# Attention, then gated attention: in Layer 1's first step, a block sum moved behind two evacuations and one group of values moved to another PSUM bank

## The chip, the core and the metric

The kernel runs on one core of a Trainium2 chip. The metric is the device time of one execution in microseconds, lower is better: before the change the median of three runs is 2317.9 us (2317.59 to 2318.22). Everything is computed in float32.

A core has a matrix engine (TensorE, "PE" in the profile, with its weight loads shown apart as "PEld"), a vector engine (VectorE, "DVE"), an activation engine (ScalarE, "ACT"), GpSimd ("POOL") and a sync engine ("SP") that here only issues DMAs. Matrix products are written to PSUM, which has eight banks; DVE and ACT read them out ("evacuate" them) to SBUF. Each engine works through its own list of instructions in order and waits at the first one whose inputs, or whose place to write, are not free.

## The reference

Eight images of 32 by 32 positions with 256 channels go through two layers.

```python
# layer 0, for each image: N = 1024 rows, C = 256, four heads
qkv = einsum('bnc,cd->bnd', xf, W_qkv)            # q, k, v for each head
atten = softmax(einsum('bihd,bjhd->bijh', q, k) * C ** -0.5, axis=2)
res = einsum('bijh,bjhd->bihd', atten, v)
x = einsum('bnd,dc->bnc', res, W_out) + b_out + xf
# layer 1, for each image: Ck = 32
f, g, h = x @ Wf + bf, x @ Wg + bg, x @ Wh + bh
o = softmax(g @ f.T, axis=-1) @ h
y = gamma * o + x
```

## The kernel before

**Tiling.** `P` is 128, `NB` 512 and `NBLK` 2: the 1024 rows of an image are worked in two blocks of 512 query columns. The loop over `steps` takes one step for every image, head and block of Layer 0, and for every image and block of Layer 1. `behind(b)` says where Layer 1 of image b-1 is put among the heads of image b: after two heads, and for the last image after all four. So seven of the eight images have the two Layer 1 steps in this loop; the last image's Layer 1 runs after it. The "first step of Layer 1" below is the step with `blk == 0`.

**Layer 0's products.** Scores, output products, projections and queries go through `seven`: a product of two matrices cut into two by two blocks is done with seven block products instead of eight. The sums of blocks that this needs are made ahead of time by `sum_a` (S1 to S4) and `sum_b` (T1 to T4), on DVE. `seven` returns three parts. The first does products 1, 6 and 5 into banks x, y and z and copies x to `e` (ACT); the second does products 2 and 7, copies x out (ACT), and adds `v` = y + e and output 22 = z + v (DVE); the third does products 4 and 3 on top of y and z and adds outputs 21 and 12 (DVE). The products add into the same banks from part to part, so that a part's products cannot start before the part ahead has read the bank.

**The projection** (`Layer0.project`, profile names ending in `_o`) uses `seven` with `two_banks=True`: x lies in one bank of the pool "psm", y and z share the other, each with 256 of its 512 columns. "psm" has two banks, so for as long as a projection is under way it holds both. All other banks, six, are the pool "ps", which scores, output products, queries and Layer 1's row products take turns in.

**Sums for the output products** (`Layer0.sums`): four pieces make S1 to S4 of the exponentiated scores, each 128 by 1024 elements on DVE. S2 and S4 share a place: S4 = a12 - S2 is written over S2, which product 6 reads in the first part of the output products; S4 itself is read by product 3, in their third part. Behind the pieces come four `keys`: three adds (L619) of S1's and S4's rows into `rs`, and `last`, one more add (L623), an all-reduce over partitions on POOL (L625) and two small DMAs on SP (`line`, L629, and `st`, L632). In a later step `invert` (L641) takes the reciprocal and sends it round through two more DMAs (L646 and L648) to become `invb`, by which the projection's outputs are multiplied (L699) before POOL adds them to `x1T` by DMA (L702).

**Layer 1's values** (`project_rows`, called by `Layer1.values`, names `pr_v_l`): four groups, each of eight matmuls of 128 by 256 into one bank, evacuated by one DVE instruction (L794).

**The order of the work.** For PE, DVE and ACT the order is written by hand: in each step, `put(tasks, *at)` collects tasks with a place number each, all of the step's tasks are sorted by it (those with the same number in the order in which they were put), and called. SP's and POOL's orders come from the framework's own scheduler. In a first step of Layer 1 the places around the change are these; "one" is the step before, "two" the step before that, both of Layer 0.

| place | task |
|---|---|
| 0 | third part of two's output products |
| 0.5, 2.4 | scores of this step, eight banks of "ps" in all |
| 0.8, 2.2, 3.5, 5.5 | S1, S2, S3, S4 of one |
| 1, 2.3, 3, 6.5 | the four groups of values |
| 1.1, 1.2, 1.3, 2.5 | block sums for two's projection |
| 2.5, 2.9, 4.2, 5.1 | transposes of Layer 1's rows (DVE, L394) |
| 4, 5 | first and second part of one's output products |
| 4.5, 6, 7.2 | the three parts of two's projection |
| 6.3, 7.6, 8.3, 8.7 | the keys of one |

The third part of one's output products is at 0 of the next step, Layer 1's second; there the scores follow at 0.5 and the first row product (`pa_l`, L899) at 1.

Of the kernel before, what the change touches and what calls it, by code (L numbers as in the profile page):

```python
# [16 lines left out]
P = 128  # L17
# [3 lines left out]
def kernel(  # L21
# [58 lines left out]
    NT = N // P  # L80
    NB = 512
# [29 lines left out]
    def tile_of(tag, shape, name):  # L111
        return pools[tag].tile(shape, F32, tag=tag, name=name)
# [244 lines left out]
    def transpose_rows(b, src, dst, layer):  # L357


        def task(k, c):  # L360
            if b not in dst:
                dst[b] = tile_of("xT", [P, CC, N], f"x{layer}T_{b}")
            pt = tile_of("psm", [P, NB], f"px{layer}_{b}_{k}_{c}")
            for t in range(HT):
                nc.tensor.transpose(
                    pt[:, ts(t, P)], src[b][:, k * HT + t, ts(c, P)], ident
                )
            nc.scalar.copy(dst[b][:, c, ts(k, NB)], pt)

        return [partial(task, k, c) for k in range(NBLK) for c in range(CC)]  # L370
# [50 lines left out]
    def key_sums(b):  # L421

        made = {}

        def piece(i):
            if i == 0:
                xT = xT_of[b]
                t = tile_of("v", [P, 4, HN], f"xs_{b}")
                sums = [t[:, k, :] for k in range(4)]
                blocks = [xT[:, c, ts(k, HN)] for k in range(2) for c in range(CC)]  # L430
                made["l"] = sum_a(sums, *blocks)
                xblocks[b] = a_operands(blocks, sums)
            made["l"][i]()

        return [partial(piece, i) for i in range(4)]
# [47 lines left out]
            partial(task, k, d) for k in range(NBLK) for d in range((width + P - 1) // P)  # L483
        ]

    def project_rows(name, w, src, evacuate):


        def task(t2):
            pm = tile_of("psm", [P, NB], f"pr_{name}_{t2}")  # L490
            for j in range(2):
                for c in range(CC):
                    nc.tensor.matmul(  # L493
                        pm[:, ts(j, C)],
                        lhsT=src()[:, c, ts(2 * t2 + j, P)],
                        rhs=w()[:, c, :],
                        start=(c == 0),
                        stop=(c == CC - 1),
                    )
            evacuate(t2, pm.rearrange("p (t c) -> p t c", c=C))  # L500

        return [partial(task, t2) for t2 in range(NT // 2)]

    def values_tile(name):
        return tile_of("v", [P, NT, CV], name)

    def ones(v):
        nc.gpsimd.memset(v[:, :, C : C + 1], 1.0)
# [208 lines left out]
    class Layer1:  # L717
# [65 lines left out]

            return [task], [partial(move, r) for r in range(quarters)]

        def values(self):
            def start():
                if self.v is None:
                    self.v = values_tile(f"v_{self.name}")
                ones(self.v)  # L790

            return [start] + project_rows(
                f"v_{self.name}", lambda: wh_sb, lambda: x1T_of[self.b],
                lambda t2, pm: nc.vector.scalar_tensor_tensor(  # L794
                    self.v[:, 2 * t2 : 2 * t2 + 2, :C], pm, gamma_sb,
                    bh_sb.unsqueeze(1).broadcast_to([P, 2, C]), ALU.mult, ALU.add,
                ),
            )

        def scores(self, blk):  # L800
# [144 lines left out]
    pm = tile_of("psm", [P, NB], "pm_idle")  # L945
# [6 lines left out]
    def behind(b):  # L952

        return 2 if b < B - 1 else HEADS
# [12 lines left out]
    turn_x, sums = transpose_rows(0, rows, xT_of, 0), key_sums(0)  # L967
# [5 lines left out]
    def is_l0(s):  # L973
        return s is not None and isinstance(s[0], Layer0)

    def step(k):
        return steps[k] if 0 <= k < len(steps) else None
# [4 lines left out]
    for i, (a, blk) in enumerate(steps):  # L982
        l0 = isinstance(a, Layer0)
        one, two, nxt = step(i - 1), step(i - 2), step(i + 1)
        places = []

        def put(tasks, *at):
            assert len(tasks) == len(at)
            places.extend(zip(at, range(len(places), len(places) + len(at)), tasks))

        if l0:
            put(a.scores(blk), 0, 2, 4, 6, 8, 10)
        else:
            tasks, _ = a.scores(blk)
            put(tasks, *((0.5, 2.4) if blk == 0 else (0.5, 2)))
        if is_l0(two):
            u, k = two
            put(u.products_of[k][2:], 1 if l0 else 0)
            if nxt is None:
                put([partial(u.invert_all, k)], 2.2)  # L1000
            put([partial(u.invert, k)], 3.4 if l0 else 2.7)
            ysums, tasks, adds[i] = u.project(k)
            put(ysums, *((1.1, 1.2, 1.3, 3.3) if l0 else (1.1, 1.2, 1.3, 2.5) if blk == 0 else
                         (0.6, 0.7, 0.8, 0.9)))
            put(tasks, *((3, 5.5, 7) if l0 else (4.5, 6, 7.2) if blk == 0 else
                         (3, 5, 7) if nxt else (1.9, 3.1, 4.1)))
            if nxt is None:
                put(adds[i], 4.2)
        if i - 1 in adds:
            put(adds[i - 1], 0.5 if l0 or blk == 1 else 2.3)  # L1010
        if is_l0(one):
            u, k = one
            sums, keys = u.sums(k)
            u.products_of[k] = u.products(k)
            put(sums, *((2.1, 3.2, 4.2, 5.6) if l0 else (0.8, 2.2, 3.5, 5.5)))
            put(keys, *((6.3, 6.6, 7.6, 8.7) if l0 else (6.3, 7.6, 8.3, 8.7)))
            put(u.products_of[k][:2], *((5, 9) if l0 else (4, 5)))
        elif one is not None:
            put(one[0].products(one[1]), *((3, 5, 7, 9) if l0 else (1, 4, 6, 8) if nxt else (1, 3, 4, 8.5)))
        if i == 0:  # L1020
            put(fold[0][2:] + fold[1], -2, -1, 0.5, 1.5, 2.5, 4.5, 6.5, 8.5)
            put(first_sums[:2], 8.4, 9.4)
        if i == 1:
            put(first_sums[2:], 1.4, 3.4)
            put(fold[2], 0.5, 2.6, 3.5, 5.5, 7.5)
            put([partial(nc.vector.tensor_scalar, bh_sb, bh_sb, gamma_sb, None, ALU.mult)], 8.5)

        if l0 and blk == 0:
            put(a.query_sums(1), 3.5, 4.3, 4.4, 5.3)
        if is_l0(nxt) and blk == NBLK - 1:  # L1030
            put(nxt[0].queries(), *((2.5, 4.5, 6.5) if not l0 else
                                    (1.5, 2.5, 4.5) if is_l0(two) else (0.5, 2.5, 5.5)))
            put(nxt[0].query_sums(0), *((6.7, 6.9, 7.3, 7.6) if not l0 else
                                        (5.4, 6.4, 7.2, 7.4) if is_l0(two) else (6.4, 7.2, 7.3, 7.4)))

        if l0 and a.h == 0 and blk == 1:
            put(residual(a.b), 5.3, 7.3)
        if l0 and a.h == 0 and blk == 1 and a.b > 0:
            put(value_sums(a.b), 1.4, 2.4, 3.4, 4.4)
        if l0 and a.h == 1 and blk == 0 and a.b + 1 < B:  # L1040
            load_x(a.b + 1)
        if is_l0(nxt) and nxt[0].h == 2 and nxt[1] == 0 and nxt[0].b + 1 < B:
            moves, turned = turn_rows(nxt[0].b + 1)
            put(moves[:4], 1, 2.5, 4, 5.5)
        if l0 and a.h == 2 and a.b + 1 < B:
            if blk == 0:
                put(moves[4:], 0.5, 1.5, 2.5, 3.5)
                put(turned, 6.4, 7.4, 8.4, 9.4)
            else:
                put(key_sums(a.b + 1), 0.5, 0.6, 6.4, 7.4)  # L1050

        if l0 and a.b > 0 and a.h == behind(a.b) - 1:
            if blk == 0:
                moves, turned1 = turn_back(a.b - 1)
                put(moves[:4], 3, 4.5, 6, 7.5)
            else:
                put(moves[4:], 4, 5.5, 7, 8.5)
                tasks, moves = nxt[0].queries_apart()
                put(tasks, 1.5)
                put(moves, 1.6, 1.7, 1.8, 1.9)  # L1060
        if not l0 and blk == 0:
            put(a.values(), 0.9, 1, 2.3, 3, 6.5)
            put(turned1, 2.5, 2.9, 4.2, 5.1)
        if nxt is None:
            fg = final.queries()
            moves, turned1 = turn_back(B - 1)
            put(moves, *[9.1 + 0.1 * k for k in range(8)])
        for _, _, t in sorted(places, key=lambda x: x[:2]):
            t()
# [90 lines left out]
    with tc.If(bad > 0), ExitStack() as general:  # L1160
# [7 lines left out]
        for b in range(B):  # L1168
# [3 lines left out]
            for h in range(HEADS):  # L1172
                a = General0(b, h, bout_sb)
# [4 lines left out]
            a = Layer1(b)  # L1178
# [37 lines left out]
```

## Time and profile before

| | us |
|---|---|
| median of three runs | 2317.9 |
| the profiled execution's own time | 2317.2 |
| its span on the core | 2315.4 |
| PE busy | 2302.4 (99%) |
| PE weight loads busy | 1892.5 (82%) |
| DVE busy | 1661.6 (72%) |
| ACT busy | 585.5 (25%) |
| POOL busy | 317.9 (14%) |
| seven instructions S4, one for each first step, mean of one | 1.2 |

The profile is one execution. "Busy" counts the time in which an engine has an instruction; the matmuls overlap, so PE's share says little about how well it is used. In the timeline, a line gives start, length, engine, source line, operation, what is written from what, shapes and count; neighbours of one kind are merged, and a bracket at the end tells how long the engine stood idle before and for whom. In a list of waits, a line gives the engine and its waiting line, whom it waited for, the total in us, how often, and the longest. Lines of helpers stand for many places: L255 is every product of `seven`, L272 every add of it, so the names of the tiles tell them apart (`_y` output products, `_o` projection, `_q` queries, no ending for scores).

### The profile page before, as it was taken

The numbers are of one execution on the slowest core, as the hardware profiler recorded it, in microseconds if no ns is written. First come the engines' busy times: TensorE is split into PE (matmuls) and PEld (weight loads), VectorE is DVE, ScalarE is ACT, GpSimd is POOL, SyncE is SP. The second block draws the span as 40 slices with busy tenths as digits, with TensorE's granted clock in tenths as the row PEclk, the third lists the DMA queues.
The fourth block names the chain that finished last, engine by engine and source line by source line (L and its number), as shares of the span: only waits on it lengthen the run. The fifth ranks groups of instructions, "written<-read, shape, count | busy, mean of one in ns | idle before, by whom it ended". The sixth has DMA issues, their size and how long they took to land.

```text
span 2315.4 us, 27268 instructions
## 1 busy us (share of the span) xinstructions
PE 2302.4 (99%) x10256; PEld 1892.5 (82%) x10256; DVE 1661.6 (72%) x2963; ACT 585.5 (25%) x1015; POOL 317.9 (14%) x199
## 2 busy tenths in 40 slices
PE   9999999999999999999999999999999999999999
PEld 7888887788878888788887888878888788888877
DVE  6787786577865777657776677766777667777765
ACT  2222222222221222212232122221222222222223
POOL 0111112011120112101121011210112101111210
PEclk9999999999999999999999999999999999999999
DMA  4211122301232012221132211321113210121222
GB/s 137 33 28 26 21 39 51 74 14 28 36 53 66 14 28 49 45 60 14 28 56 42 57 15 28 58 42 55 19 24 58 42 36 19 28 46 24 39 44 49
DMA packets 239740, 94.16 MB, mean 41 GB/s; under 512 B 204208, under 2 KB 208944, under 8 KB 239600
## 3 DMA queue, kind: packets, MB, share of 16 engines
q1 hardware_dynamic: 220400, 55.10, 12.2%
q0 software_dynamic: 19200, 37.23, 9.2%
q8 instruction: 83, 1.36, 0.4%
q14 instruction: 57, 0.47, 0.1%
HBM read 29.76 MB, written 8.65 MB: 17 GB/s over the span
## 4 chain that ended last, share of the span: by engine, by line
PE 98%; DVE 1%; issue 0%; ACT 0%; DVEq 0%
PE psy_y L255 14%; PE psy L255 14%; PE pa_l L899 10%; PE psx L255 10%; PE psz L255 10%; PE psx_y L255 10%; PE psz_y L255 10%; PE psy_o L255 6%; PE psy_q L255 4%; PE psx_q L255 2%; PE psz_q L255 2%; PE psx_o L255 2%; PE pr_v_l L493 2%; PE ps_l L811 1%; PE pm_fg L766 1%; DVE ss L612 0%
## 5 line engine op out<-in xcount | busy, mean ns | idle before, releaser
L625 POOL PARTITION_ALL_REDUCE rb<-rs x64 | 206.6, 3229 | 1450.8 <-DVE rs L623 910.1
L255 PE MATMUL psx<-q,x0T 128*128 128x256 f32 x1024 | 263.5, 380 | 0.0
L255 PE MATMUL psy<-qs,xs 128*128 128x256 f32 x1024 | 262.9, 379 | 0.0
L255 PE MATMUL psz<-q,xs 128*128 128x256 f32 x1024 | 262.8, 379 | 0.0
L575 ACT ACTIVATE p<-p 128x1024 f32<-128x1024 f32 x128 | 135.3, 1057 | 494.0 <-DVE p L272 494.0
L255 PE MATMUL psx_y<-p,x 128*128 128x256 f32 x1024 | 241.9, 379 | 0.0
L255 PE MATMUL psy_y<-p,xt 128*128 128x256 f32 x1024 | 241.9, 379 | 0.0
L899 PE MATMUL pa_l<-v_l,s_l 128*128 128x257 f32 x1024 | 231.5, 381 | 0.0
L255 PEld LDWEIGHTS psx<-q,x0T 128*128 128x128 f32 x1024 | 193.8, 190 | 45.3 <-issue 20.7
L255 PEld LDWEIGHTS psx_y<-p,x 128*128 128x128 f32 x1024 | 194.6, 190 | 34.1 <-issue 8.6
L899 PEld LDWEIGHTS pa_l<-v_l,s_l 128*128 128x128 f32 x1024 | 193.9, 190 | 32.9 <-issue 6.1
L255 PEld LDWEIGHTS psy<-qs,xs 128*128 128x128 f32 x1024 | 194.5, 190 | 26.8 <-DVE q L272 0.4
L255 PEld LDWEIGHTS psz<-q,xs 128*128 128x128 f32 x1024 | 194.6, 190 | 26.5
L255 PEld LDWEIGHTS psy_y<-p,xt 128*128 128x128 f32 x1024 | 194.6, 190 | 26.5
L284 ACT ACTIVATE p<-psx 128x512 f32<-128x512 f32 x128 | 76.5, 597 | 363.7 <-PE psx L255 363.5
L272 DVE TENSOR_TENSOR u<-psy,e 128x512 f32<-128x512 f32 x128 | 88.2, 689 | 87.0 <-ACT e L278 75.5
L702 POOL DMA_DIRECT2D x1T<-o x64 | 78.0, 1219 | 424.2 <-DVE o L699 301.8
L255 PE MATMUL psy<-qs,x0T 128*128 128x256 f32 x512 | 132.1, 380 | 0.3 <-DVE v L272 0.3
L272 DVE TENSOR_TENSOR v<-psy,e 128x512 f32<-128x512 f32 x128 | 88.3, 690 | 52.8 <-PE psy L255 51.3
L255 PE MATMUL psy_y<-ss,xt 128*128 128x256 f32 x512 | 121.4, 380 | 0.1
L255 PE MATMUL psz_y<-ss,x 128*128 128x256 f32 x512 | 121.0, 379 | 0.0
L255 PE MATMUL psz_y<-ss,xt 128*128 128x256 f32 x512 | 120.9, 379 | 0.0
(141 smaller groups left out, 3418.5 us busy)
## 6 DMA issues: line engine op xcount, KB each, us to landing
x1T<-o POOLq DMA_DIRECT2D x64, 512.0 KB, 5.0
invb<-inv SPq DMA_DIRECT2D x63, 256.0 KB
x<-x1T SPq DMA_DIRECT2D x256, 32.0 KB
out_dram<-x SPq DMA_DIRECT2D x15, 512.0 KB
x<-in_x_dram SPq DMA_DIRECT2D x14, 512.0 KB
x0T<-x SPq DMA_DIRECT2D x224, 32.0 KB
fg<-v_l POOLq DMA_DIRECT2D x56, 64.0 KB, 2.1
w<-in_L_conv_W_qkv_dram SPq DMA_DIRECT2D x4, 512.0 KB
```

The costliest lines, as they stand in the source:

```text
L255: nc.tensor.matmul(banks[k][:, ts(i, w)], lhsT=lhsT, rhs=rhs, start=first and n == 0, stop=True, skip_group_check=True,)
L272: nc.vector.tensor_tensor(dst, shaped(banks[k]), shaped(other), ALU.add)
L284: copy(outs["11"](), shaped(banks["x"]))
L493: nc.tensor.matmul(pm[:, ts(j, C)], lhsT=src()[:, c, ts(2 * t2 + j, P)], rhs=w()[:, c, :], start=(c == 0), stop=(c == CC - 1),)
L575: exp(both, both)
L625: nc.gpsimd.partition_all_reduce(t, r.rearrange("p e i -> p (e i)"), P, bass_isa.ReduceOp.add)
L702: nc.gpsimd.dma_start(x1T_of[self.b][:, :, ts(blk, NB)], o, accum_op=ALU.add)
L766: nc.tensor.matmul(pm[ts(k, half)], lhsT=w[:, c, :], rhs=x1T_of[b][:, c, ts(k, NB)], start=(c == 0), stop=(c == CC - 1),)
L811: nc.tensor.matmul(pm, lhsT=self.f[ts(r, CK), ts(j0 + r, P)], rhs=self.g[ts(r, CK), ts(blk, NB)], start=True, stop=True,)
L899: nc.tensor.matmul(pm[:, : C + 1], lhsT=p[:, j, ts(ti, P)], rhs=v[:, j, : C + 1], start=(j == 0), stop=(j == NT - 1),)
```

## The change

Three things change, in the first steps of Layer 1 only.

- S4 moves from place 5.5 to 6.1. It was ahead of the projection's second part (6) and is now behind it, ahead of the first of the keys (6.3).
- `project_rows` gets an argument `last`, the pool of its last group's bank, and `values` hands it on. Without it nothing is different.
- The loop's call of `values` gives "ps": the fourth group of values (place 6.5) takes one of the six banks of the scores instead of one of the two of "psm".

```diff
-    def project_rows(name, w, src, evacuate):
+    def project_rows(name, w, src, evacuate, last="psm"):
         def task(t2):
-            pm = tile_of("psm", [P, NB], f"pr_{name}_{t2}")
+            tag = "psm" if t2 < NT // 2 - 1 else last
+            pm = tile_of(tag, [P, NB], f"pr_{name}_{t2}")
...
-        def values(self):
+        def values(self, last="psm"):
...
                     bh_sb.unsqueeze(1).broadcast_to([P, 2, C]), ALU.mult, ALU.add,
-                ),
+                ), last,
             )
...
-            put(sums, *((2.1, 3.2, 4.2, 5.6) if l0 else (0.8, 2.2, 3.5, 5.5)))
+            put(sums, *((2.1, 3.2, 4.2, 5.6) if l0 else (0.8, 2.2, 3.5, 6.1)))
...
         if not l0 and blk == 0:
-            put(a.values(), 0.9, 1, 2.3, 3, 6.5)
+            put(a.values("ps"), 0.9, 1, 2.3, 3, 6.5)
```

The `put` of the sums is reached only where the step before is one of Layer 0, and of Layer 1's steps that is the first alone. The values of the last image, after the loop, and the kernel's general path, which runs only if a check of the sums fails, call without the argument and stay as they were.

## The prediction

> **What bounds the kernel now.** I read the page first, then the waits by engine, then the timeline of one first step of Layer 1 on TensorE, on its weight loads, and on VectorE. The page:
>
> ```profile
> span 2315.4 us, 27268 instructions
> PE 2302.4 (99%) x10256; PEld 1892.5 (82%) x10256; DVE 1661.6 (72%) x2963; ACT 585.5 (25%) x1015; POOL 317.9 (14%) x199
> ```
>
> TensorE (PE) has 13 us of the span not busy, and its waits are few. The list of waits, PE and its loads:
>
> ```profile
> PE psy_o L255 <- DVE o L272: 4.2, 7, 0.6
> PE pm_idle L947 <- DVE col L134: 1.1, 1, 1.1
> ...
> PEld psy_o L255 <- DVE o L272: 7.0, 7, 1.0
> ...
> PEld pr_v_l L493 <- ACT o L284: 3.0, 7, 0.4
> ```
>
> The largest wait comes seven times, once in each of the seven first steps of Layer 1 in the loop over steps. All seven look alike; I take the first (372 to 404 us). Columns: start, length, engine. PE, then its loads, then VectorE (DVE):
>
> ```profile
> 394.24 0.59 PE L255 MATMUL psx_o<-y,wvo 128*128 128x256 f32 x2
> 394.67 0.59 PE L255 MATMUL psy_o<-yt,wo 128*128 128x256 f32 x2
> 395.29 1.99 PE L493 MATMUL pr_v_l<-wh_sb,x1T 128*128 128x256 f32 x8
> 397.89 0.70 PE L255 MATMUL psy_o<-yt,wvo 128*128 128x256 f32 x2 [0.61 <-DVE o L272]
> 398.43 0.59 PE L255 MATMUL psy_o<-y,wo 128*128 128x256 f32 x2
> ```
> ```profile
> 395.29 1.59 PEld L493 LDWEIGHTS pr_v_l<-wh_sb,x1T 128*128 128x128 f32 x8 [0.43 <-ACT o L284]
> 397.89 0.30 PEld L255 LDWEIGHTS psy_o<-yt,wvo 128*128 128x128 f32 x2 [1.01 <-DVE o L272]
> ```
> ```profile
> 394.44 0.42 DVE L272 TENSOR_TENSOR v_y<-psy_y,e_y 128x256 f32<-128x256 f32 x1 [2.96 <-PE psy_y L255]
> 394.90 0.43 DVE L272 TENSOR_TENSOR y<-psz_y,v_y 128x256 f32<-128x256 f32 x1
> 395.24 0.70 DVE L394 STREAM_TRANSPOSE x<-x 128x512 f32<-128x512 f32 x1
> 395.86 1.18 DVE L612 TENSOR_TENSOR ss<-p,ss 128x1024 f32<-128x1024 f32 x1
> 396.97 0.41 DVE L272 TENSOR_TENSOR v_o<-psy_o,e_o 128x256 f32<-128x256 f32 x1
> 397.42 0.42 DVE L272 TENSOR_TENSOR o<-psy_o,v_o 128x256 f32<-128x256 f32 x1
> ```
>
> L612 at 395.86 is S4. It stands ahead of v_o and o, the two evacuations after the projection's second part. PE is in order: its third part (397.89) loads 0.05 us after the end of o (397.84).
>
> **What the Trainium skill says.** "PSUM — Partial Sum Buffer", section on bank collisions, says that PSUM is to be guarded by bank and quadrant, not by address. The trace agrees: the third part's first product writes only the y half, read by v_o (ended 397.38), yet is released by o, the reader of the z half of the same bank. "SBUF — State Buffer", section "Who interferes with whom", says that a VectorE instruction with two SBUF inputs contends with a GpSimd instruction that reads SBUF. The trace agrees: the multiply at 402.86 beside the all-reduce (401.78 to 405.01) took 2.23 us; most others take 1.22.
>
> **The change part by part.**
>
> *(a) S4 from 5.5 to 6.1.* It passes only what the projection's second part (at 6) issues: PE's four matmuls and ACT's copy are not in its queue; on DVE it passes v_o and o. It issues no DMA, and no SP or POOL instruction of its own stands between. Now v_o takes S4's slot, 395.86 (product 7 ended at 395.26); o follows 0.45 later as today, 396.31 to 396.73; PE may load at 396.78 instead of 397.89. S4's start-to-start time is 1.11 us (395.86 to 396.97), so o comes 1.11 us earlier.
>
> *(b) The last values' group in a bank of the scores.* The projection with two_banks holds both psm banks (x in one, y and z in the other). So the fourth group today waits until ACT has copied x out: its load comes 0.43 us late, its matmuls at 395.29 instead of 394.67 + 2 x 0.216 = 395.10. In a ps bank that wait goes; the new one is on that bank's last reader. Counting allocations in program order (the bank longest free is given), it is the bank of the sixth score block of this step, exponentiated by 384.6: over for 10 us. The next score blocks then get the four oldest free banks in shifted order; the values' own bank is the fourth, evacuated about 399.1 and wanted about 401.3. Cost nothing; the cover is 2 us.
>
> *(c) Sum.* PE's group of eight takes 8 x 0.216 = 1.73 (as every group of eight at 1.73 between starts), 395.10 to 396.83, so (b) lets PE arrive in time for o, and (a) sets the end: the load at 396.78, then the pair at 0.54 (397.89 to 398.43, a pair that starts without a preloaded weight; others 0.43). The pair ends its turn at 397.32 instead of 398.43: **1.11 us per step**. Alone, (a) would let PE go on at 397.12, where it is ready today: 0.77 to 0.88; (b) alone nothing, since o ends at 397.84 anyway. Upper end: all that is lost now, 0.19 + 0.10 (the group at 1.83) + 0.77 + 0.11 = 1.17. Seven steps: 7 x 1.11 = 7.8 us.
>
> *What is late next.* With PE 1.11 us earlier I check each thing it then meets; DVE has the same work, so its clock hardly moves.
> - S4 ends about 397.85; the product that reads it (400.59 now) comes at 399.48: 1.4 us of cover.
> - The first add of S4's rows now stands right behind S4 and depends on it: a dependent pair starts 0.46 apart (394.44, 394.90), an independent one 0.34, so DVE is about 0.12 later. The add out of psy_y, now 401.52, ends at 402.06; pa_l takes that bank, at 403.48 - 1.11 = 402.37. Cover 0.3 us. Without it PE would stand by what is missing, before each of seven steps.
> - The multiply by invb ends with the all-reduce, near 405.1, early or not. Four ysums and the first row's reciprocal and add follow, until about 407.5; psy_q, which by the same count of banks takes pa_l's, loads at 408.75 - 1.11 = 407.64. Cover 0.1. In the seventh step the projection comes sooner (2238.66 - 1.11 = 2237.55, ysum ended at 2237.51): some 0.1 to 0.2 us lost once.
> - DMAs do not follow PE: the sums' columns land at 412.4, invb at 431.8, and DVE stands for them (0.83 and 1.40 us today). Behind invb stands v (ends 433.66), for which PE loads at 435.32, then at 434.21: cover 0.55 in the first batch. In the other five v ends near 432.96 on the same scale (717.32 + 0.69 - 285.05): 1.2.
>
> So 7.8 less about 0.1: **7.7 us**. Profiled execution 2317.2 (span 2315.4 and 1.8 around it) becomes 2309.5; it stood 0.7 below the median of the runs, so the median 2317.9 becomes **2310.2**.
>
> **The rivals.**
>
> *B, part of the gain.* The waits' list of PE names only 0.61 us a step; taken so, 4.3 us, 2313.6. Against it: the loads' 1.01 and 0.43 are gaps of the same place, and PE's starts account for 1.17. Nearer is that a thin cover fails, pa_l's 0.3 or psy_q's 0.1: every missing tenth costs 0.7 us, and three tenths give 2312.3.
>
> *C, no change.* If the group were handed another bank than I count, the next scores could draw the bank of psz_y, which DVE empties only near 402.5, while PE wants it at 401.3: 1.2 us back per step, about 2318. For it: the trace shows no bank numbers. Against: the order of frees in the code leaves the four other banks older.
>
> *D, slower.* SP's order is not written by hand. The moves of the next x0T wait for the last values' group to let go of x1T (SP's first starts at 397.32, the group ends 397.28), and it now ends about 0.3 earlier. If more of them were put ahead of the sums' DMAs, invb would land later and PE stand at v. A move takes about 0.63 us of SP (3 in 1.89, 7 in 4.59). PE loses 6 x (delay - 1.1, the mean cover), and it is slower by over 0.2% when this exceeds 7.7 + 4.6, from a delay of 3.2 us, five moves. Eight moves, 5.0 us, cost 23.4: 2333.6. Against: SP now stands from 401.9 to 405.0 for the all-reduce; four or five moves that slip in there cost nothing.
>
> **How the numbers follow.** A measurement of this kernel tells 0.2%, 4.6 us, from no change. A, the forecast, 0.74 (2309.4 to 2311.2: 1.17 a step at one end, 0.95 at the other); B 0.14 (2311.2 to 2314, mostly still faster); C 0.08; D 0.04. Faster: 0.74 and 0.12 of B, 0.86; same: 0.10; slower 0.04. The range 2309.3 to 2313.0 holds A but its edges and most of B.
>
> **What would show it.** Right: PE's wait of psy_o for o gone or below 0.2 us a step; pr_v's wait for ACT gone; DVE in the order v_o, o, S4, first add, values; the distance from psx_o's second pair to the first pa_l in that step 1.1 us shorter, and the period of a batch (first pr_v to first pr_v) 283.95 instead of 285.07 us. Wrong: a new PE wait at pa_l (for y), at ps_l (for y or z), or at psy (for v) with a longer DVE wait for invb.

## The result, and the profile after

The changed kernel takes 2311.62 us (median of eight runs, 2311.16 to 2312.06); the kernel before, run beside it, took 2318.06 us. The ratio is 0.9974, with an interval of 0.9965 to 0.9983: 6.4 us faster, where 7.7 were forecast. The profiled execution took 2311.8 us, with a span of 2309.9.

The page of the kernel after:

```profile
span 2309.9 us, 27289 instructions
PE 2299.7 (100%) x10256; PEld 1891.9 (82%) x10256; DVE 1663.3 (72%) x2963; ACT 585.5 (25%) x1015; POOL 317.9 (14%) x199
```

The waits of PE, of its loads and of DVE, kernel after (total, times, longest). The diff moves the lines from 490 on down by one: L493, L612 and L699 of before are L494, L613 and L700 here.

```profile
PE psy L255 <- DVE v L272: 1.6, 4, 0.5
...
PEld psy L255 <- DVE v L272: 6.1, 12, 0.9
...
PEld psy_o L255 <- DVE o L272: 1.4, 7, 0.3
...
DVE o L700 <- DMA invb<-inv: 20.8, 6, 3.9
```

PE's wait of `psy_o` for `o`, 4.2 us in all before, is not in its list any more. In its place stands a small wait that hardly existed before (0.3 us, once): `psy`, a product of Layer 0's scores, for the evacuation `v`. And DVE stands 20.8 us for `invb`, not 4.5.

First, the place of the change: the timeline of the first step of Layer 1, kernel after.

```profile
393.72 0.59 PE L255 MATMUL psx_o<-y,wvo 128*128 128x256 f32 x2
394.15 0.59 PE L255 MATMUL psy_o<-yt,wo 128*128 128x256 f32 x2
...
394.58 1.89 PE L494 MATMUL pr_v_l<-wh_sb,x1T 128*128 128x256 f32 x8
394.72 0.70 DVE L394 STREAM_TRANSPOSE x<-x 128x512 f32<-128x512 f32 x1
395.34 0.39 DVE L272 TENSOR_TENSOR v_o<-psy_o,e_o 128x256 f32<-128x256 f32 x1
...
395.76 0.42 DVE L272 TENSOR_TENSOR o<-psy_o,v_o 128x256 f32<-128x256 f32 x1
396.11 1.22 DVE L613 TENSOR_TENSOR ss<-p,ss 128x1024 f32<-128x1024 f32 x1
396.24 0.30 PEld L255 LDWEIGHTS psy_o<-yt,wvo 128*128 128x128 f32 x2 [0.17 <-DVE o L272]
396.31 0.64 PE L255 MATMUL psy_o<-yt,wvo 128*128 128x256 f32 x2
```

The values' group starts 0.43 us after the pair before it, without a wait for ACT's copy; S4 stands behind `o`; the load of the third part comes 0.06 us after the end of `o` (396.18). That this first product, which writes only the y half, still goes by the reader of the z half agrees again with what the Trainium skill says in "PSUM — Partial Sum Buffer" on bank collisions. (The two halves are also slices of one tile of the program, and no run here tells a guard by bank from a guard by tile.) From this step's second pair of `psx_o` to its first `pa_l` it is 8.11 us (393.72 to 401.83); before it was 9.24 (394.24 to 403.48). Six of the seven steps show 8.11, one (the third) 8.27: 7.75 us in all, or 7.9 without the 0.16 that the third lost to a late transfer (see e1); 7.8 were forecast.

Now the place that gives some of it back, 38 us later in Layer 0. The timeline of the kernel before, DVE and PE, then that of the kernel after, DVE, PE and its loads:

```profile
431.84 1.23 DVE L699 TENSOR_TENSOR o<-o,invb 128x1024 f32<-128x1024 f32 x1 [1.40 <-DMA invb<-inv]
432.98 0.68 DVE L272 TENSOR_TENSOR v<-psy,e 128x512 f32<-128x512 f32 x1
...
435.53 1.03 PE L255 MATMUL psy<-qs,x0T 128*128 128x256 f32 x4
```
```profile
432.46 1.23 DVE L700 TENSOR_TENSOR o<-o,invb 128x1024 f32<-128x1024 f32 x1 [3.68 <-DMA invb<-inv]
433.61 0.68 DVE L272 TENSOR_TENSOR v<-psy,e 128x512 f32<-128x512 f32 x1
...
434.34 0.73 PEld L255 LDWEIGHTS psy<-qs,x0T 128*128 128x128 f32 x4 [0.70 <-DVE v L272]
434.35 0.91 PE L255 MATMUL psy<-qs,x0T 128*128 128x256 f32 x3 [0.30 <-DVE v L272]
```

DVE stands for `invb` with the multiply at the head of its list; `v`, which needs nothing of it, is queued behind, and PE's next `psy` waits for `v`. A batch is the stretch from one image's first group of values (`pr_v_l`) to the next one's; the table counts us from each first group on. The forecast's own numbers give 54.6 as the latest start of the multiply that costs nothing (load 434.21, less 0.05, less 1.82 from the multiply's start to the end of `v`, less 377.76). The same working with the figures of the profile after gives 54.65:

| batch | 1 | 2 | 3 | 4 | 5 | 6 |
|---|---|---|---|---|---|---|
| multiply by `invb` starts, before | 54.1 | 53.3 | 53.2 | 53.2 | 53.5 | 53.3 |
| the same, after | 55.22 | 54.77 | 55.58 | 54.35 | 55.36 | 54.99 |
| period, after, over the best of 283.93 (sixth: 404.74) | 0.57 | 0.11 | 0.92 | 0 | 0.71 | 0.33 |

The last row is the second less 54.65, where that is positive, to within 0.01. Its sum is 2.64 us, 0.16 of it in the projection of batch 3. The account of the two profiled executions: 7.9 gained, 2.6 lost here, 0.3 lost in the seventh step (below), 0.5 ahead of the loop's first group of values, which starts at 377.24 instead of 377.76: 5.5, as 2317.2 less 2311.8 gives 5.4. The 0.5 is not the change's: in the twelve profiles of this case that group starts between 377.1 and 378.3.

### The profile page after: what moved, and what is told of

Read it like the earlier page. It is cut to its first block, busy times and chain, and to the rows that moved or that the text cites. A ratio compares the mean times of both kernels' runs of the same rounds, so it can differ in the third digit from the quotient of the medians.

```text
span 2309.9 us, 27289 instructions
## 1 busy us (share of the span) xinstructions
PE 2299.7 (100%) x10256; PEld 1891.9 (82%) x10256; DVE 1663.3 (72%) x2963; ACT 585.5 (25%) x1015; POOL 317.9 (14%) x199
## 4 chain that ended last, share of the span: by engine, by line
PE 96%; DMA 3%; DVE 1%; SPq 0%; ACT 0%; issue 0%; DVEq 0%
PE psy_y L255 14%; PE psy L255 14%; PE psx_y L255 10%; PE psz_y L255 10%; PE psz L255 9%; PE psx L255 9%; PE pa_l L900 8%; PE psy_o L255 6%; PE psy_q L255 3%; PE pr_v_l L494 3%; PE psx_q L255 2%; PE psx_o L255 2%; PE psz_q L255 2%; DMA inv<-inverse 2%; PE ps_l L812 1%; DMA invb<-inv 1%
## 5 line engine op out<-in xcount | busy, mean ns | idle before, releaser
L272 DVE TENSOR_TENSOR v<-psy,e 128x512 f32<-128x512 f32 x128 | 88.3, 690 | 53.0 <-PE psy L255 51.7
```

Source lines behind the costliest of these rows:

```text
L272: nc.vector.tensor_tensor(dst, shaped(banks[k]), shaped(other), ALU.add)
```

## The experiments

Ten runs were made in three groups, e1 to e4, e5 to e8, and e9 with e10, each group on its own chip; e8 and e9 repeat the kernels before and after. Each ratio is to the kernel before in the same group. The theory: S4's place ahead of the evacuations sets PE's restart, the bank only lets PE get there in time, and what was missing went at `invb`. The rivals: the bank does the work; SP's order puts more transfers ahead of `invb`; the landing of `invb` differs by itself, with no edit, and the loss with it.

### One part alone

**e1**, S4 moved, the bank as before:

```diff
-            put(a.values("ps"), 0.9, 1, 2.3, 3, 6.5)
+            put(a.values(), 0.9, 1, 2.3, 3, 6.5)
```

> Only S4 moved (6.1); the last values' group stays in its psm bank. Theory (S4's place sets when PE may go on, the bank only keeps PE from being late for it): the values' group still starts 0.19 us late, PE is ready at its old moment, and the distance from psx_o's second pair to the first pa_l falls from 9.24 us to 8.36 (0.88 less; 1.13 less with both). Seven times 0.88 is 6.2 us, less what is given back at invb (0.2 to 0.4 a batch): about 2313. Rival (the bank brings a share of its own, the two add up): about 8.7, and the other 0.6 shows with the bank alone.

Measured: 2314.69 us, ratio 0.9983 (0.9976 to 0.9991), 1.7 us above the 2313 expected. Five steps show 8.37 us from `psx_o` to `pa_l`, 0.87 less than before. The other two show 8.52 and 9.22; together they lose 1.0 us of the gain, and two batches lose 1.0 us each at `invb`, more than the 0.2 to 0.4 expected. The third batch, kernel e1, PE and ACT:

```profile
965.70 0.37 ACT L284 COPY o<-psx_o 128x256 f32<-128x256 f32 x1 [2.64 <-DMA x1T<-o]
...
966.13 1.99 PE L494 MATMUL pr_v_l<-wh_sb,x1T 128*128 128x256 f32 x8 [0.89 <-ACT o L284]
```

ACT's copy out of `psx_o` writes `o`, which an earlier DMA (`x1T<-o`) still reads. With both banks of "psm" held, PE stands for that copy. In the kernel after the same copy came 3.36 us late, and the step lost only 0.16 us, since DVE's `o` waited 0.19 us for the same transfer. So the bank has a second use that the forecast did not name.

**e2**, the bank changed, S4 at 5.5 as before:

```diff
-            put(sums, *((2.1, 3.2, 4.2, 5.6) if l0 else (0.8, 2.2, 3.5, 6.1)))
+            put(sums, *((2.1, 3.2, 4.2, 5.6) if l0 else (0.8, 2.2, 3.5, 5.5)))
```

> Only the last values' group in a bank of the scores; S4 stays at 5.5. Theory: nothing, since o ends when it did: the distance stays at 9.24, the values' group starts 0.2 us earlier and PE's wait for o grows from 0.61 to about 0.9 us; time 2318. Rival (the two add up): the distance falls by 0.3 to 0.6 us, time 2314 to 2316.

Measured: 2319.50 us, ratio 1.0003 (0.9995 to 1.0012), and 9.23 to 9.25 us from `psx_o` to `pa_l`: nothing gained. (The time is 1.5 us above the 2318 expected; e4 says where that went.) PE's waits, kernel e2, show where its earlier arrival goes:

```profile
PE psy_o L255 <- DVE o L272: 6.3, 7, 0.9
```

PE finishes the values sooner and stands 0.9 us a step for the same `o`, not 0.6. S4 alone brings 0.87, the bank alone 0, and both together 1.13, as the forecast's working had it (0.77 to 0.88, 0, 1.11): the rival that the bank does the work is out.

### Another dose at the same place

**e5**, the kernel before with the fourth transpose of Layer 1's rows behind the evacuations, in place of S4:

```diff
-            put(turned1, 2.5, 2.9, 4.2, 5.1)
+            put(turned1, 2.5, 2.9, 4.2, 6.05)
```

> The kernel before, with the fourth transpose (0.62 us on DVE) moved behind the projection's second part, S4 left at 5.5. Theory (PE goes on when o ends, whatever stands ahead of it on DVE): o ends 0.62 us earlier, PE's wait for o of 0.61 goes, the distance from psx_o's second pair to the first pa_l falls from 9.24 to about 8.6; seven times 0.62 is 4.3 us, less 0 to 0.3 a batch at invb: 2314 to 2316. Rival (S4 itself is the hindrance, by what it locks or reads, not its length): 9.24 stays.

Measured: 2313.56 us, ratio 0.9985 (0.9978 to 0.9991), 8.64 us from `psx_o` to `pa_l`: 0.60 less. The transpose's start-to-start time is 0.62. PE restarts directly behind `o`, kernel e5:

```profile
396.64 0.42 DVE L272 TENSOR_TENSOR o<-psy_o,v_o 128x256 f32<-128x256 f32 x1
396.98 0.70 DVE L394 STREAM_TRANSPOSE x<-x 128x512 f32<-128x512 f32 x1
397.12 0.30 PEld L255 LDWEIGHTS psy_o<-yt,wvo 128*128 128x128 f32 x2 [0.41 <-DVE o L272]
```

Two different instructions, 1.11 and 0.62 us from start to start, moved across the same two evacuations, pay 1.13 (with the bank changed too, so that PE is there in time) and 0.60. That is what the step claims.

**e6**, both behind the evacuations, and the multiply by `invb` moved as in e3 below:

> The changed kernel with the multiplication by invb at 4.5 and also the fourth transpose behind the projection's second part. Theory: o now ends before PE is ready for it, so only the last 0.06 us a step is left to gain: distance 8.05, batch periods 283.87, about 0.4 us below the same without the transpose, 2309.2. Rival (PE still waits for DVE there): 0.6 us a step, 2305.

Measured: 2310.16 us, ratio 0.9970 (0.9959 to 0.9981). A miss: 8.18 us (8.51 in the third batch, where ACT's copy was late again), not shorter than 8.11. `psy_o`'s third part does not wait for `o` any more, but the next thin cover (the time by which a result is ready before it is wanted) is used up. Kernel e6, DVE and the loads:

```profile
402.42 0.42 DVE L272 TENSOR_TENSOR y<-psy_y,e_y 128x256 f32<-128x256 f32 x1
...
402.96 1.16 PEld L900 LDWEIGHTS pa_l<-v_l,s_l 128*128 128x128 f32 x6 [0.84 <-issue]
```

The add out of `psy_y` ends at 402.84 and `pa_l` loads 0.12 us later. This is the cover that the forecast put at 0.3 (in the kernel after the add ends at 401.56, 0.27 before `pa_l` at 401.83). The likely reason, read from the timeline and not tried: DVE has no more work to put between `y` (395.46) and `v_o` (395.99), which stands for its product, and so it is about 0.2 us later. The place is worked out: 8.1 us is about what this order of DVE gives.

### Where the missing part went

**e3**, the kernel after with the multiply by `invb` later in the Layer 0 step that follows Layer 1's two:

```diff
-            put(adds[i - 1], 0.5 if l0 or blk == 1 else 2.3)
+            put(adds[i - 1], (0.5 if is_l0(one) else 4.5) if l0 else 0.5 if blk == 1 else 2.3)
```

> The changed kernel, and in the first Layer 0 step behind Layer 1 the multiplication by invb stands at 4.5 instead of 0.5, so that DVE doesn't stand for the DMA in front of the scores' v. Theory (what was given back, 2.6 us over six batches, was given back behind that wait): no PE wait of psy for v, all batch periods 283.9 us, time about 2309.0. Rival (given back to crowded DMA queues or otherwise): periods stay between 283.9 and 284.9, time 2311.6.

Measured: 2309.62 us, ratio 0.9958 (0.9941 to 0.9975); every period 283.93 us, the last 404.73. `invb` was issued no earlier than in the kernel after (at 429.05; over the six batches 49.8 to 51.8 us after the first group of values, against 49.0 to 51.7), and it cost nothing. The waits of DVE, kernel e3:

```profile
DVE o L700 <- DMA invb<-inv: 0.3, 1, 0.3
```

**e4**, the same edit on the kernel before:

> The kernel before, with the same later place of the multiplication alone. Theory: PE did not stand there before the change, so nothing: periods 285.06 us, time 2318 within 0.5. Rival (that DVE wait cost PE something already): up to 2 us faster.

Measured: 2318.12 us, ratio 0.9995 (0.9986 to 1.0003), periods 285.06: nothing that the measurement can tell. The kernel before has 1.1 us more cover at `invb`: there PE loads for `psy` at 435.32, not 434.21, so the multiply may start up to 55.7 us after the first group of values. In the two profiles of the kernel before (the first and e8) every landing stays under that. In e2, on the same chip as e4, where PE comes no earlier either, the multiply started at 56.0 to 56.5 in one batch after another and the periods were 0.2 to 0.7 us too long. The loss is thus no new mechanism; the change takes away the cover that hid it in the profile of before. On this chip the kernel before may lose there too: e3 is 9.2 us below it, more than the 7.9 of the place, but e4's interval does not tell that from nothing.

**e7**, the kernel after with the last sixteen of the next x0T's 32 moves kept behind the inverse's DMA on SP:

```diff
-                nc.sync.dma_start(line.rearrange("o (t p) -> p (o t)", p=P), inv)
+                held["inv"] = nc.sync.dma_start(line.rearrange("o (t p) -> p (o t)", p=P), inv)
...
-                put(moves[4:], 0.5, 1.5, 2.5, 3.5)
+                put([partial(behind_inverse, m) for m in moves[4:]], 0.5, 1.5, 2.5, 3.5)
```

> The changed kernel (the multiplication back at 0.5); on SP the last sixteen moves of the next x0T are held behind the DMA of the inverse, so that it is issued behind 16 of them instead of 21. Theory (invb is late because its DMAs queue behind the moves on SP): the inverse is issued about 5 us earlier in the step, invb is there before DVE wants it, no PE wait of psy for v, batch periods 283.9, 2309.6. Rival (invb is late for the all-reduce or the transfers themselves): invb comes less than 1 us earlier, periods 284 to 285.

Measured: 2309.39 us, ratio 0.9967 (0.9954 to 0.9980), periods 283.93. SP's timeline, kernel after first, then kernel e7:

```profile
408.50 9.19 SPq L386 DMA_DIRECT2D x0T<-x  x11
417.79 0.54 SPq L647 DMA_DIRECT2D inv<-inverse  x1
...
428.91 0.34 SPq L649 DMA_DIRECT2D invb<-inv  x1
```
```profile
409.06 4.84 SPq L387 DMA_DIRECT2D x0T<-x  x6
414.01 0.54 SPq L648 DMA_DIRECT2D inv<-inverse  x1
...
422.59 0.34 SPq L650 DMA_DIRECT2D invb<-inv  x1
```

With 16 moves ahead of it instead of 21 the inverse goes out 3.8 us sooner, `invb` 6.3 us sooner, and nothing waits for it. Against e6, which ran on the same chip with 21 moves ahead, it is 4.2 and 4.1 us, averaged over the six batches. Two independent remedies, one on DVE's list and one on SP's, give the same period. Neither ran beside the changed kernel in its own group. For e3 the late `invb` shows that a loss was there to take out; for e7 the trace shows only that the wait is gone, not how much the changed kernel would have lost on that chip.

**e8**, the kernel before once more, a single run:

> The kernel before once more, for its trace on this chip. If invb's landing differs by chip or run and not by the edit, its DVE wait is here above the 0.5 to 1.4 us of the first profile and periods may exceed 285.06; if it is the edit, 285.06 and the same waits.

Measured: 2317.59 us. The multiply starts 53.5 to 55.4 us after the first group of values; in the first profile of the same kernel it was 53.2 to 54.1. So in each batch it is 0.2 to 2.2 us later, with nothing changed in the kernel, and DVE stands 0.8 to 2.3 us for `invb` instead of 0.5 to 1.4: a later landing needs no edit. In one batch PE stood 1.3 us for ACT's copy, as in e1, and that step took 9.67 us instead of 9.24.

**e9**, the kernel after once more, and **e10**, with both remedies:

> The changed kernel once more, beside the next run on one chip. Theory: distance 8.11 in every first step; what it loses against 283.93 a batch differs from batch to batch with invb's landing; 2311 to 2313. Rival (the first profile of it was a chance): periods 283.93, 2309.5.

> The changed kernel with both remedies: the moves held behind the inverse's DMA and the multiplication by invb at 4.5. Theory (both take away the same loss, and there is only one): periods 283.93 as with either, 2309.5, no better than one alone. Rival (there are two losses): below 2309.

Measured: 2309.72 us for both, ratios 0.9967 (0.9954 to 0.9979) and 0.9967 (0.9955 to 0.9980), beside 2317.44 before. Kernel e9, the first batch again, DVE and PE:

```profile
431.55 1.23 DVE L700 TENSOR_TENSOR o<-o,invb 128x1024 f32<-128x1024 f32 x1 [2.62 <-DMA invb<-inv]
432.69 0.68 DVE L272 TENSOR_TENSOR v<-psy,e 128x512 f32<-128x512 f32 x1
...
434.03 1.03 PE L255 MATMUL psy<-qs,x0T 128*128 128x256 f32 x4
```

This time the multiply starts 53.4 to 54.2 us after the first group of values, always under 54.65; DVE still waits, PE does not, every period is 283.93, and the whole 7.7 us are there. The loss in each batch that was expected of e9 did not come. So the gain is 6.4 us in one measurement and 7.7 in the other, by how late `invb` lands.

Nor does that look like chance from one execution to the next. The eight runs of the first measurement lie at 2311.2 to 2312.1 us, the six of e9 at 2309.5 to 2310.0. Averaged over the six batches, the time from the issue of the inverse's DMA to that of `invb`, one profile a run, goes by the group and not by the kernel:

| profile | from the issue of `inv` to that of `invb`, mean |
|---|---|
| before, after (chips not on record) | 8.6, 9.5 |
| e1, e2, e3, e4 (one chip) | 10.1, 10.6, 10.1, 10.3 |
| e5, e6, e7, e8 (a second) | 9.0, 8.9, 9.1, 9.1 |
| e9, e10 (a third) | 8.8, 8.9 |

No run separates the chip from what else a group shares. Both remedies together show the same period as either, but as e9 had no loss on that chip, e10 had none to take out and cannot tell one loss from two. The medians of e3, e7, e9 and e10, 2309.4 to 2309.7, lie too close together to be ranked.

## Why the prediction was right, and where it was off

- **(a) and (c), S4's place: right.** 1.13 us a step against 1.11; alone 0.87, within 0.77 to 0.88; seven steps 7.9 (7.75 with the late transfer in the third) against 7.8. e5 shows the same rule with another instruction.
- **(b), the bank: right that alone it gives nothing, and that no later bank comes short (rival C is out).** "Cost nothing" was too modest: it also takes PE out of the way of a late `x1T<-o`, which cost a step 0.86 us in e1 and 0.43 in e8, and 0.16 in the kernel after.
- **"What is late next": the covers of S4's reader and of `pa_l` were right** (0.27 against 0.3); e6 shows what happens once the second is gone. The multiply beside the all-reduce ends 0.1 us after it, at 404.71, and takes 2.90 us; the Trainium skill, "SBUF — State Buffer", "Who interferes with whom", names this kind of pair as one that contends. The seventh step was named, and sized at 0.1 to 0.2; it lost 0.28 (PE gains 0.85 us there, not 1.13). The forecast held the sum's end against the start of the matmul, 2238.66; the weight load ahead of it starts at 2238.45 and has to wait for the sum too. The wait is at the projection's second pair, kernel after:

```profile
2232.56 0.42 DVE L691 TENSOR_TENSOR yt<-y 128x256 f32<-128x256 f32 x1
2233.04 0.30 PEld L255 LDWEIGHTS psy_o<-yt,wo 128*128 128x128 f32 x2 [0.42 <-DVE yt L691]
```

- **"DMAs do not follow PE": the place and the threshold were right, the size was not.** This is the term that was off. It took `invb`'s landing of one profile for a constant and left a cover of 0.55 us in the first batch and 1.2 in the others. In the next profile `invb` was ready 1.1 to 2.4 us later on the same scale, in every batch; 2.6 us went there, where nothing was put down. A spread of the landing belonged into the range and into the likeliest value; the six landings in the profile of before, 53.2 to 54.1, gave only a lower bound on it. That the likeliest value, 2310.2, lies between the two measurements (2311.6, and 2309.7 in e9) is luck in this respect: nothing in its working stood for the landing's spread.
- **Rival D named the right place; its cause is not what the traces show.** Its chain (later `invb`, DVE at the multiply, `v` behind it, PE at `psy`) is what the trace shows. But SP had 21 moves ahead of the inverse in every batch, not more than the 22 of before. Counted from the first group of values and averaged over the six batches, the multiply starts 1.6 us later than before: 0.3 of it because the inverse is issued later, 0.9 in the inverse's transfer (from its issue to that of `invb`), and 0.4 between the issue of `invb` and the multiply. In the first batch the transfer takes 9.0 us before, 11.1 after, 10.5 in e9, 9.4 in e8, 8.6 in e7. **What makes this transfer vary stays open;** the table under e9 shows that it goes with the group of runs, and e7 that its place on SP decides when it starts.
- **Rival B** came out in size (2311.6), not in mechanism: `pa_l`'s cover held, and at `psy_q` the loads come 0.57 us apart (406.56, 407.13) where they came 0.54 apart (408.21, 408.75), by which PE loses nothing: in the fourth batch, where `invb` cost nothing, the period is the full 1.13 us shorter.

## What to carry to other kernels

When PE waits for an evacuation, look at what stands ahead of that evacuation on its engine: moving an instruction behind it paid its start-to-start time here, once per place, as far as the next thin cover. Then list the events that do not move with PE, DMA landings above all, for which the evacuating engine stands in order with PE's next evacuation behind: their cover shrinks by all that is gained, and it must be held against their spread over several profiles, from more than one group of runs, and not against one. Here such a wait was cheap to take out, by moving the consumer back or by putting the urgent small transfer ahead of the bulk ones in the queue.

## What the runs showed of the hardware that was not expected

- The inverse's DMA moves 2 KB, four floats from each of 128 partitions into single places of a row, and takes 8.1 to 12.8 us until the next transfer is issued behind it (six batches in each of the twelve profiles). In the chain of waits of the kernel after, from 372 to 440 us, it is the longest piece:

```profile
417.79 11.05 DMA inv<-inverse
```

The Trainium skill, "DMA: Bandwidth & Descriptors", "Rules for kernel authors", says that a non-contiguous last dimension lowers to one descriptor per element and is better rearranged; the time here fits with that, but no run tried it in another layout.

- The transfer `x1T<-o` holds up ACT's copy in a batch now and then (2.64 us in e1, 3.36 in the kernel after, 3.49 in e2), and not at all in most. With the bank changed, PE does not stand for that copy, and the wait shows in no list of PE.
